# Eight key and value products of layer 1 moved into the end of layer 0's attention, and routing in one pass

## The chip, the cores and the metric

The kernel runs on one core of a Trainium2 chip. The metric is the time of one execution on the device in microseconds (us). TensorE is PE in the profile (PEld is its weight load), VectorE is DVE, ScalarE is ACT, GpSimd is POOL, and SyncE (SP) issues most DMAs.

## The reference

Two layers over 16 blocks (b = 0 to 15) of 128 tokens of width 512, all in float32. Each layer is a cross attention, added to the tokens, and then a mixture of eight experts of which each token takes two, added again.

```python
# layer 0
x = x + attention0(layernorm(x), ctx)      # fp8-rounded self attention and cross attention
t = layernorm(x)                           # written to x0_dram, what the experts read
probs = softmax(t @ Wg); gate, expert = top_k(probs, 2)
x = x + sum of gate * (relu(t[expert's tokens] @ w1) @ w2)      # at most 640 tokens an expert
# layer 1, per block b
h = layernorm(x[b])
k = concat(ctx[b] @ Wk, h @ Wk)            # 128 context rows, 128 own rows
v = concat(ctx[b] @ Wv, h @ Wv)
q = h @ Wq                                 # 16 heads of 128, four groups for k and v
k, q = rope(rms_norm(k)), rope(rms_norm(q))
x = x + softmax(q k^T / sqrt(128)) v @ Wo
x = x + two experts of eight on layernorm(x), weighted by softmax of the top two logits
```

`ctx` is an input: the products `ctx[b] @ Wk` and `ctx[b] @ Wv` of layer 1 depend on nothing that layer 0 makes.

## The kernel before

There are four stages, one after the other: layer 0's attention (0 to about 1368 us of the profiled execution), its experts (to 2408), layer 1's attention (to about 3474) and its experts (to 3819).

**Order.** Within a stage PE, DVE, ACT and POOL run in the order that the Python code is written in (`InOrder`, line 67, wraps every call; therefore nearly all instructions carry L67 in the profile). DMAs on SP are placed by the framework's scheduler. Tiles come from pools; a new tile waits until the memory that it gets is no longer used, also by tiles of a pool that was closed before.

**Layer 0's attention** (`Layer0`) goes over 64 token blocks n: four quarters (half of the heads of cross or self attention each) of 16 blocks. `ORDER` lists the steps of a period as (step, lag): step `name` of block n is issued in period n + lag, so that up to nine blocks are in flight. Steps are named by what they do: `Kp`, `Vp`, `Qp` project, `po0`, `po1` are the output projection into one PSUM bank, `xr` adds it to the tokens, `rn1` ... `rtb` are the routing steps. Weights are prepared in pieces into the pool tag `w`, 28 units of 4 KB per partition. After n = 63 the pipeline runs dry: in periods 64 to 71 fewer and fewer steps are left, at the end only routing.

**Routing** (`Routing`, lines 174 to 319) is the same in both layers. For each block of 128 tokens:
- `rl`, `rmx`, `rex`, `rch` (logits, top, exps, choice): logits on PE, then the two best experts and their weights on DVE, and a mask of 128 x 8.
- `rpl` (ranks): two small f32 matmuls, a triangle of ones (`before`) with the mask, and ones with `macc`, the masks of earlier blocks summed.
- `rsl` (slots): DVE makes each token's slot in its expert, and adds the mask to `macc`.
- `rlh` (onehots): `r_one` and `r_two` by six DVE operations of 128x128, for each of the two choices one for the slot's one half, and two for its other half, times the token's number and times its weight.
- `ren`, `rtb` (entry, entered): the matmul of `r_one` and `r_two`, 256 columns in f32 (token numbers and weights), added into `r_table` by DVE.

In layer 0 routing runs in quarter 3 alone; the last blocks are 60 to 63.

**Layer 0's experts** (`Experts0`) begin with `slot_rows` (line 924 on): DVE makes `e_ids`, `e_source` and `e_target` out of `r_table`. POOL then gathers the first expert's token blocks `g` by `e_source`, PE transposes them, and `h` (first matmul) and `o` (second) follow for eight experts. `rows_behind` sets `e_zero` and writes it to DRAM. Tiles for layer 1's weights (`c_wq`, `c_wk`, `c_wv`, `c_wo`) lie in a pool of their own; the list `ahead` loads them during the experts.

**Layer 1's attention** (`Layer1`) has its own list `ORDER1` with lags 0 to 8 over 16 blocks; a period takes about 64.2 us. `Kp0`/`Vp0` project the context's key and value (r = 0; `Kp1`/`Vp1` the tokens' own), each four f32 matmuls of 128x512; `Ksq0`, `Krs0`, `Kn0` normalise the key, `V0` copies the value from PSUM to SBUF. `AHEAD` issues these for b = 0 and 1 before period 0. In a period the order around the change is

```python
("QT0", 4), ("Qa1", 4), ("Vp0", 4), ("Qs1", 4), ("rn1", 6),
("sc10", 4), ("PT02", 5), ("pn3", 5), ("Kp0", 3), ("V0", 4), ("lnn", 3), ("sc00", 4),
("nm10", 4), ("rp1", 6), ("Ksq0", 3), ("trX", 3),
```

so Kp0 of block b runs in period b + 3, and Vp0 in period b + 4. `lnn` writes `xn` on DVE, and `trX` transposes it on PE.

Of the kernel before, what the change touches and what calls it, by code (L numbers as in the profile page):

```python
# [11 lines left out]
F32 = mybir.dt.float32  # L12
# [11 lines left out]
P = 128  # L24
# [32 lines left out]
class InOrder:  # L57


    def __init__(self, tc, engine):  # L60
        self.tc, self.engine = tc, engine
# [19 lines left out]
class Ops:  # L81


    def __init__(self, nc, tc, const):
        self.nc, self.tc, self.uid = nc, tc, 0
        self.ident = self.t(const, [P, P], F32, "ident")
        make_identity(nc, self.ident)
        self.ones = self.t(const, [P, P], F32, "ones")
        nc.gpsimd.memset(self.ones, 1.0)

        self.before = self.t(const, [P, P], F32, "before")
        nc.gpsimd.affine_select(
            out=self.before, in_=self.ones, pattern=[[1, P]], compare_op=ALU.is_gt,
            fill=0.0, base=0, channel_multiplier=-1,
        )
        self.iota = self.t(const, [P, P], F32, "iota")
        nc.gpsimd.iota(
            self.iota, pattern=[[1, P]], base=0, channel_multiplier=0,
            allow_small_or_imprecise_dtypes=True,
        )  # L100
        self.tok = self.t(const, [P, NB], F32, "tok")
        nc.gpsimd.iota(
            self.tok, pattern=[[P, NB]], base=0, channel_multiplier=1,
            allow_small_or_imprecise_dtypes=True,
        )
        self.tok1 = self.t(const, [P, NB], F32, "tok1")
        nc.gpsimd.iota(
            self.tok1, pattern=[[P, NB]], base=1, channel_multiplier=1,
            allow_small_or_imprecise_dtypes=True,
        )  # L110
        self.mhalf = self.t(const, [P, 16], F32, "mhalf")
        nc.gpsimd.memset(self.mhalf, -0.5)
# [33 lines left out]
class Router:  # L146
# [5 lines left out]

    def __init__(self, ops, pool, x_dram, w, probs, hi_first, rows, turned):
        nc = ops.nc
        self.ops, self.pool, self.x_dram = ops, pool, x_dram
        self.w, self.probs, self.hi_first = w, probs, hi_first

        self.rows, self.turned = rows, turned  # L160
        t = ops.t
        self.macc = t(pool, [P, E], F32, "r_macc")
        nc.gpsimd.memset(self.macc, 0.0)
        self.table = t(pool, [P, 2 * P], F32, "r_table")
        nc.gpsimd.memset(self.table, 0.0)
        self.weight = t(pool, [P, NB, 2], F32, "r_weight")
        self.expert = t(pool, [P, NB, 2], F32, "r_expert")
        self.pos = t(pool, [P, NB, 2], F32, "r_pos")
        self.onehot = t(pool, [P, NB, 2, E], F32, "r_onehot")
        self.base = t(pool, [P, E], F32, "r_base")  # L170
        nc.vector.tensor_scalar(self.base, ops.iota[:, :E], float(SPAN), None, ALU.mult)


class Routing:
# [61 lines left out]
    def choice(self):  # L236

        r, j, v, mx, s1 = self.r, self.j, self.v, self.mx, self.s1
        nc = r.ops.nc
        wt = r.weight[:, j, :]  # L240
        if r.probs:
            nc.vector.reciprocal(s1[:, 2:3], s1[:, 1:2])
            nc.vector.tensor_scalar(v, v, s1[:, 2:3], None, ALU.mult)
            nc.vector.max(mx, v)
            nc.vector.tensor_copy(wt, mx[:, 0:2])
        else:
            nc.vector.tensor_scalar(s1[:, 2:3], s1[:, 1:2], 1.0, None, ALU.add)
            nc.vector.reciprocal(wt[:, 0:1], s1[:, 2:3])
            nc.vector.tensor_tensor(wt[:, 1:2], s1[:, 1:2], wt[:, 0:1], ALU.mult)
        ix = self.tile([P, E], U32, "r_ix", 2)  # L250
        nc.vector.max_index(ix, mx, v)
        ex = r.expert[:, j, :]
        nc.vector.tensor_copy(ex, ix[:, 0:2])
        oh = r.onehot[:, j, :, :]
        for k in range(2):
            nc.vector.tensor_scalar(
                oh[:, k, :], r.ops.iota[:, :E], ex[:, k : k + 1], None, ALU.is_equal
            )
        self.mask = self.tile([P, E], F32, "r_mask", 2)
        nc.vector.tensor_tensor(self.mask, oh[:, 0, :], oh[:, 1, :], ALU.add)  # L260

    def ranks(self):
        ops = self.r.ops
        self.pp = ops.t(self.psum, [P, D], F32, "mm")
        ops.nc.tensor.matmul(self.pp[:, :E], ops.before, self.mask, start=True, stop=False)
        ops.nc.tensor.matmul(self.pp[:, :E], ops.ones, self.r.macc, start=False, stop=True)

    def slots(self):

# [22 lines left out]
    def onehots(self):  # L292
        r, j = self.r, self.j
        nc, iota = r.ops.nc, r.ops.iota
        first, second = (1, 0) if r.hi_first else (0, 1)
        self.one = self.tile([P, 2, P], F32, "r_one", 1)
        self.two = self.tile([P, 2, 2 * P], F32, "r_two", 1)
        for k in range(2):
            a, b = (self.lohi[:, i, k : k + 1] for i in (first, second))
            nc.vector.tensor_scalar(self.one[:, k, :], iota, a, None, ALU.is_equal)  # L300
            for i in range(2):
                by = r.weight[:, j, k : k + 1] if i else r.ops.tok1[:, j : j + 1]
                nc.vector.tensor_scalar(
                    self.two[:, k, i * P : (i + 1) * P], iota, b, by, ALU.is_equal, ALU.mult
                )

    def entry(self):
        r = self.r
        self.pt = r.ops.t(self.psum, [P, D], F32, "mm")
        for k in range(2):  # L310
            r.ops.nc.tensor.matmul(
                self.pt[:, : 2 * P], self.one[:, k, :], self.two[:, k, :],
                start=(k == 0), stop=(k == 1),
            )

    def entered(self):

        r = self.r
        r.ops.nc.vector.tensor_tensor(r.table, r.table, self.pt[:, : 2 * P], ALU.add)


def project(ops, psum, xT, w, cols):
# [14 lines left out]

WEIGHTS = ("k", "q0", "v", "q1", "p0", "p1")
BANKS0 = {"mm": 3, "tr": 2, "sc": 1, "pv": 1, "po": 1}

# [36 lines left out]
class Layer0:  # L377
# [9 lines left out]

    def __init__(self, ops, tc, args, x_dram, vec, router, small, wpool, work, dram, banks):  # L390
        self.plain, self.tc = ops.nc, tc
        ops.nc = Engines(tc, ops.nc)
        nc, t = ops.nc, ops.t
        self.ops, self.args, self.x_dram, self.vec, self.router = ops, args, x_dram, vec, router
        self.wpool, self.work, self.banks = wpool, work, banks

        self.kept = {
            kind: [t(dram, [P, D], F32, f"kept_{kind}{b}") for b in range(NB)]
# [249 lines left out]
    def load(self, n):  # L648
# [15 lines left out]
        if quarter in (1, 3):  # L664
            s["xq"] = t(work, [P, NC, P], F32R, "xq", 3)
            self.fetch("q" if quarter == 3 else "qx", b, s["xq"])

    def load_v(self, n):
        ops, t, s = self.ops, self.ops.t, self.at[n]
        quarter, b = divmod(n, NB)  # L670
# [205 lines left out]
    def run(self):  # L876
        lags = {name: lag for name, lag in ORDER}
        count = 0
        for period in range(4 * NB + max(lags.values())):
# [5 lines left out]
            for i, (name, lag) in enumerate(ORDER):  # L885
                if 0 <= period - lag < 4 * NB:
                    self.step(name, period - lag)
                count += 1
                if count % 3 == 0 and (period % NB < 7 or count % 2 == 0):
                    self.weight_step()  # L890
# [2 lines left out]
        self.ops.nc = self.plain  # L893


def layer0_attention(ops, tc, args, x_dram, vec, router):
    with ExitStack() as ctx:
        small = ctx.enter_context(tc.tile_pool(name="a_small", bufs=1))
        wpool = ctx.enter_context(tc.tile_pool(name="a_w", bufs=1))
# [5 lines left out]
            def tile(self, shape, dt, name, tag, bufs=None):  # L905
                return psum.tile(shape, dt, name=name, tag=tag, bufs=BANKS0[tag])

        Layer0(ops, tc, args, x_dram, vec, router, small, wpool, work, dram, Banks()).run()


def gather(ops, out, table, index):
# [289 lines left out]
class Layer1:  # L1201
# [8 lines left out]
    )  # L1210

    def __init__(self, ops, args, x_rows, w, rope_dram, router, out, first, work, banks):
        self.ops, self.args, self.x_rows, self.rope_dram = ops, args, x_rows, rope_dram
        self.first = first
        self.wq, self.wk, self.wv, self.wo = w
        self.router, self.out, self.work, self.banks = router, out, work, banks
        self.at = [{} for _ in range(NB)]
# [1 line left out]
    def load_first(self, b):  # L1219

        t, nc, s = self.ops.t, self.ops.nc, self.at[b]
        s["cT"] = t(self.first, [P, NC, P], F32, "cT", 2)
        nc.sync.dma_start(out=s["cT"], in_=self.args["ctxT"][b])
        s["rp"] = t(self.first, [P, 3, 2, P], F32, "rp", 3)
        nc.sync.dma_start(out=s["rp"].rearrange("p i s h -> p (i s h)"), in_=self.rope_dram[b])

# [82 lines left out]
    def key_step(self, name, r, b, s):  # L1309
        ops, nc, t = self.ops, self.ops.nc, self.ops.t  # L1310
        src = s["hT"] if r and name in ("Kp", "Vp") else s["cT"]
        if name == "Kp":
            s["ps", "k", r] = project(ops, self.banks, src, self.wk, slice(0, D))
        elif name == "Vp":
            s["vp", r] = project(ops, self.banks, src, self.wv, slice(0, D))
# [101 lines left out]
                self.at[period - last].clear()  # L1417


def layer1_attention(ops, tc, args, x_rows, w, rope_dram, router, out, first):  # L1420
    with ExitStack() as ctx:
        work = ctx.enter_context(tc.tile_pool(name="c_work", bufs=1))
        psum2 = ctx.enter_context(tc.tile_pool(name="c_ps", bufs=2, space=PSUM))
# [7 lines left out]
                return pool.tile(shape, dt, name=name, tag=tag)  # L1431

        scheduled, ops.nc = ops.nc, Engines(tc, ops.nc)
        Layer1(ops, args, x_rows, w, rope_dram, router, out, first, work, Banks()).run()
        ops.nc = scheduled


class Blocks1:
# [43 lines left out]
    def tables(self, small):  # L1482
# [4 lines left out]
        self.block0 = self.slots(small, ops.ident[:, 0:1], 1, "e0")  # L1487
        self.gather(0, self.at[0])
        pc = t(self.psum, [P, D], F32, "po")
        nc.tensor.matmul(pc[:, :E], ops.ones, router.macc, start=True, stop=True)  # L1490
        count = t(small, [P, E], F32, "count")

        nc.vector.tensor_scalar(count, pc[:, :E], 1.0, None, ALU.max)
# [149 lines left out]
def xattn_moe_two_layers(ctx: ExitStack, tc: tile.TileContext, args, out):  # L1643
# [21 lines left out]
    router0 = Router(ops, rpool0, x0_dram, wr[:, 0], True, False, ("xn", 2), ("lnT", 2))  # L1665
    router1 = Router(ops, rpool1, x1_dram, wr[:, 1], False, True, ("r_xn", 1), ("r_xT", 1))

    layer0_attention(ops, tc, args, x_rows, vec, router0)

    with tc.tile_pool(name="c_w", bufs=1) as wpool:  # L1670
        wq = t(wpool, [P, NC, NH * P], F32, "c_wq")
# [4 lines left out]
        def ahead(work):  # L1676
# [10 lines left out]

        layer0_experts(ops, tc, args, router0, x0_dram, x_dram, out, wpool, ahead)
        layer1_attention(
            ops, tc, args, x_rows, (wq, wk, wv, wo), rope_dram, router1, out, wpool  # L1690
        )
    layer1_experts(ops, tc, args, router1, x1_dram, out)

# [71 lines left out]
```

## Time and profile before

| | |
|---|---|
| median of three runs | 3816.66 us (3816.5 to 3819.55) |
| profiled execution | 3821.12 us, of which the span of the trace is 3819.4 |
| granted PE clock, mean | 0.971 |
| PE, DVE, ACT, POOL busy | 94%, 48%, 37%, 32% |
| layer 0's attention ends, e_ids starts | 1368.23 |
| first expert matmul h | 1388.42 |
| HBM traffic | 231.72 MB read, 78.92 MB written |

An f32 matmul is two instructions in the trace, an FP32R matmul one. A timeline line reads: start in us, duration in us, engine, line, operation, tile written <- tiles read, shape, count of like instructions in a row, and in brackets the engine's idle time before it with what ended it. The count of instructions and the busy time are given for each engine in the windows.

### The profile page before, as it was taken

What the parts mean: (1) busy time and instruction counts of PE and PEld (TensorE: products, weight loads), DVE (VectorE), ACT (ScalarE), POOL (GpSimd) and SP (SyncE); (2) the same over time, 40 slices, a digit from 0 to 9 for tenths busy, and PEclk for the clock granted to TensorE, in tenths of its full rate; (3) what the DMA queues carried; (4) which work ended last, traced back from release to release, by engine and by line L of the source; (5) the groups of instructions that cost most, each with busy time, mean ns of one, the idle gap of its engine ahead of it and who ended that gap; (6) DMA issues with size and microseconds to landing.
All of it is one profiled execution on the core that took longest, in us unless ns stands there. A gap on an engine that the chain in (4) does not pass through costs nothing. (4 is left out here: it accounts for less than half of the span.)

```text
span 3819.4 us, 42132 instructions
## 1 busy us (share of the span) xinstructions
PE 3597.5 (94%) x13349; PEld 2165.4 (57%) x13349; DVE 1838.0 (48%) x4269; ACT 1406.4 (37%) x5153; POOL 1214.3 (32%) x1487
## 2 busy tenths in 40 slices
PE   5999899889899869999999999899999999998998
PEld 3666566667688745444444444355555555554565
DVE  6888888778788923200000000255555555553111
ACT  5666555666676501101100000243434343441111
POOL 7546655654532202211001100332222222221332
PEclk8999899999899979999999999999999999998999
DMA  4333333333322163433233331200101010005333
GB/s 157 112 96 115 110 111 108 111 102 97 111 86 89 53 229 117 116 91 102 81 95 94 91 83 33 46 21 23 32 23 32 23 32 20 20 9 225 67 67 53
DMA packets 135412, 313.55 MB, mean 82 GB/s; under 512 B 15944, under 2 KB 16072, under 8 KB 133392
## 3 DMA queue, kind: packets, MB, share of 16 engines
q1 hardware_dynamic: 117488, 269.28, 21.9%
q0 software_dynamic: 17696, 41.43, 5.6%
q8 instruction: 119, 1.95, 0.2%
q14 instruction: 109, 0.89, 0.1%
HBM read 231.72 MB, written 78.92 MB: 81 GB/s over the span
## 5 line engine op out<-in xcount | busy, mean ns | idle before, releaser
L67 PE MATMUL h<-xT,w 128*128 128x512 f32 x1024 | 466.3, 595 | 5.1 <-PEq L1112 2.5
L67 PE MATMUL o<-w,hT 128*128 128x512 f32 x1024 | 460.8, 592 | 0.0
L67 ACT ACTIVATE hT<-h 128x512 f32<-128x512 f32 x128 | 76.3, 596 | 861.4 <-PE h L67 861.4
L67 DVE COPY xT<-tr 128x512 f32<-128x512 f32 x79 | 54.4, 688 | 593.9 <-PE tr L67 593.9
L67 PEld LDWEIGHTS o<-w,hT 128*128 128x128 f32 x1024 | 194.2, 190 | 243.7 <-issue 242.5
L67 PEld LDWEIGHTS h<-xT,w 128*128 128x128 f32 x1024 | 189.3, 190 | 233.3 <-issue 231.7
L67 PE MATMUL mm<-w,xq 128*128 128x512 f32 x1024 | 296.2, 434 | 24.5 <-DVE xq L67 7.0
L67 ACT ACTIVATE p<-sc,sm_nm 128x128 f32<-128x128 f32 (+1 forms) x768 | 300.9, 408 | 26.3 <-DVE sm_nm L67 15.7
L67 PE MATMUL sc<-kT,qT 128*128 128x128 f32 (+1 forms) x1536 | 267.6, 311 | 8.2 <-ACT p L67 5.5
L67 PE MATMUL pv<-pT,v 128*128 128x256 f32 (+1 forms) x768 | 258.5, 460 | 1.6 <-ACT pT L67 1.4
L67 PEld LDWEIGHTS sc<-kT,qT 128*128 128x128 f32 x1536 | 222.4, 191 | 66.3 <-issue 44.5
L67 ACT ACTIVATE hn_sq<-mm 128x128 f32<-128x128 f32 x768 | 213.2, 278 | 125.6 <-PE mm L67 104.9
L67 POOL DMA_INDIRECT x_dram<-y,e_target x40 | 62.9, 1574 | 574.7 <-ACT y L67 564.9
L67 PEld LDWEIGHTS mm<-w,xq 128*128 128x128 f32 x1024 | 199.0, 202 | 77.6 <-issue 10.0
L67 PE MATMUL mm<-c_wq,hT 128*128 128x512 f32 x512 | 231.2, 594 | 0.7 <-DVE qn L67 0.7
L67 PE MATMUL po<-c_wo,oT 128*128 128x512 f32 x512 | 231.4, 595 | 0.0
L67 DVE TENSOR_REDUCE sm_nm<-sc 128x4 f32<-128x512 f32 (+1 forms) x256 | 176.0, 687 | 114.0 <-PE sc L67 111.9
L67 POOL TENSOR_TENSOR hn_rs<-hn_rs,mhalf 128x4 f32<-128x4 f32 x192 | 202.8, 1056 | 16.0
L67 PE MATMUL h<-e_w,xT 128*128 (+1 forms) x624 | 201.8, 467 | 4.1 <-issue 3.3
L67 PE MATMUL po<-w,cq 128*128 128x512 f32 x512 | 184.2, 441 | 22.5 <-DVE cq L67 3.4
L67 POOL TENSOR_SCALAR hn_rs<-hn_ss,ws 128x4 f32<-128x4 f32 x160 | 70.1, 438 | 420.0 <-ACT hn_sq L67 419.7
L67 PE MATMUL tr<-ident,p 128*128 128x128 f32 x1024 | 157.1, 280 | 48.1 <-DVE p L67 40.8
(234 smaller groups left out, 6441.6 us busy)
## 6 DMA issues: line engine op xcount, KB each, us to landing
w<-in_f_w SPq DMA_DIRECT2D x128, 512.0 KB
x_dram<-xr SPq DMA_DIRECT2D x64, 256.0 KB
xr<-x_dram SPq DMA_DIRECT2D x64, 256.0 KB
e_w<-in_f_w SPq DMA_DIRECT2D x8, 1408.0 KB
xk<-in_ctxT SPq DMA_DIRECT2D x32, 256.0 KB
xv<-in_ctxT SPq DMA_DIRECT2D x32, 256.0 KB
raw<-in_wproj SPq DMA_DIRECT2D x32, 256.0 KB
lnT<-kept_lnT SPq DMA_DIRECT2D x32, 256.0 KB
```

Of the source, the lines that this page charges most:

```text
L67: return self.tc.keep_in_program_order(call(*args, **kwargs))
```

## The change

It has three parts.

1. **Early products.** When `Vp` of the last block of layer 0's attention has been issued, `load_early` loads Wk and Wv of layer 1 (four halves in `w` units) and the contexts of b = 2 to 5 (in the buffers `xk` and `xv`). `follow` then issues their eight products (K and V of four contexts) on PE behind steps of block 63: two after `po1`, one after `rl`, one after `rpl`, four after `ren`. Each is copied by ACT into a `v` tile and stored to `kv_dram` (256 KB) by SP.
2. **Layer 1** reads them back. For b = 2 to 5 Kp0 issues no matmul: the tile `cT` now holds the key product, loaded from DRAM, and Ksq0 and Kn0 read it from SBUF. Vp0 is a DMA straight into the tile `v`, and V0 does nothing.
3. **Routing in one pass**, in both layers. Mask, `macc`, `before` and ones of the ranks are bf16. `r_one` and `r_two` are FP32R. The weights are cut into two halves (two small DVE operations in `choice`), so `r_two` has 384 columns instead of 256. Its four weight one-hots are made on POOL; DVE keeps two for the token numbers and two for `r_one`. `entered` has a second DVE addition.

```diff
@@ Ops, Router
-        self.before = self.t(const, [P, P], F32, "before")
+        self.ones_b = self.t(const, [P, P], BF16, "ones_b")
+        nc.gpsimd.memset(self.ones_b, 1.0)
+        self.before_b = self.t(const, [P, P], BF16, "before_b")
...
-        self.macc = t(pool, [P, E], F32, "r_macc")
+        self.macc = t(pool, [P, E], BF16, "r_macc")
@@ Routing.choice
-        self.mask = self.tile([P, E], F32, "r_mask", 2)
+        self.mask = self.tile([P, E], BF16, "r_mask", 2)
...
+        half = self.halves = self.tile([P, 2, 2], F32, "r_halves", 2)
+        nc.vector.tensor_scalar(
+            half[:, 0, :].bitcast(U32), wt.bitcast(U32), 12, 12, ALU.logical_shift_right,
+            ALU.logical_shift_left,
+        )
+        nc.vector.tensor_tensor(half[:, 1, :], wt, half[:, 0, :], ALU.subtract)
@@ Routing.ranks
-        ops.nc.tensor.matmul(self.pp[:, :E], ops.before, self.mask, start=True, stop=False)
-        ops.nc.tensor.matmul(self.pp[:, :E], ops.ones, self.r.macc, start=False, stop=True)
+        ops.nc.tensor.matmul(self.pp[:, :E], ops.before_b, self.mask, start=True, stop=False)
+        ops.nc.tensor.matmul(self.pp[:, :E], ops.ones_b, self.r.macc, start=False, stop=True)
@@ Routing.onehots
-        self.one = self.tile([P, 2, P], F32, "r_one", 1)
-        self.two = self.tile([P, 2, 2 * P], F32, "r_two", 1)
+        self.one = self.tile([P, 2, P], F32R, "r_one", 1)
+        self.two = self.tile([P, 2, 3 * P], F32R, "r_two", 1)
...
+            nc.vector.tensor_scalar(
+                self.two[:, k, :P], iota, b, r.ops.tok1[:, j : j + 1], ALU.is_equal, ALU.mult
+            )
             for i in range(2):
-                by = r.weight[:, j, k : k + 1] if i else r.ops.tok1[:, j : j + 1]
-                nc.vector.tensor_scalar(
-                    self.two[:, k, i * P : (i + 1) * P], iota, b, by, ALU.is_equal, ALU.mult
+                nc.gpsimd.tensor_scalar(
+                    self.two[:, k, (i + 1) * P : (i + 2) * P], iota, b,
+                    self.halves[:, i, k : k + 1], ALU.is_equal, ALU.mult,
                 )
@@ Routing.entry, entered
-                self.pt[:, : 2 * P], self.one[:, k, :], self.two[:, k, :],
+                self.pt[:, : 3 * P], self.one[:, k, :], self.two[:, k, :],
...
+        weights = r.table[:, P:]
         r.ops.nc.vector.tensor_tensor(r.table, r.table, self.pt[:, : 2 * P], ALU.add)
+        r.ops.nc.vector.tensor_tensor(weights, weights, self.pt[:, 2 * P : 3 * P], ALU.add)
@@ Layer0
+EARLY = (2, 3, 4, 5)
+EARLY_AFTER = {"po1": 2, "rl": 1, "rpl": 1, "ren": 4}
...
+    def load_early(self):
+        nc, t = self.ops.nc, self.ops.t
+        assert not self.pieces and self.units >= 4
+        self.early_w, self.early = [], []
+        for w in (self.args["Wk"], self.args["Wv"]):
+            halves = [t(self.wpool, [P, 2, D], F32, "w", W_UNITS) for _ in range(2)]
+            for i, half in enumerate(halves):
+                nc.sync.dma_start(out=half, in_=w[:, 2 * i : 2 * i + 2, :])
+            self.early_w.append(halves)
+        for k, b in enumerate(EARLY):
+            cT = t(self.work, [P, NC, P], F32, "xv" if k % 2 else "xk", 2)
+            nc.sync.dma_start(out=cT, in_=self.args["ctxT"][b])
+            self.early += [(b, i, cT) for i in range(2)]
+
+    def early_product(self):
+        nc, t = self.ops.nc, self.ops.t
+        b, i, cT = self.early.pop(0)
+        ps = t(self.banks, [P, D], F32, "mm")
+        for c in range(NC):
+            nc.tensor.matmul(
+                ps, cT[:, c, :], self.early_w[i][c // 2][:, c % 2, :],
+                start=(c == 0), stop=(c == NC - 1),
+            )
+        out = t(self.work, [P, D], F32, "v", 3)
+        nc.scalar.copy(out, ps)
+        nc.sync.dma_start(out=self.kv_dram[b][i], in_=out)
+
+    def follow(self, name):
+        if name == "Vp":
+            self.load_early()
+        for _ in range(EARLY_AFTER.get(name, 0)):
+            self.early_product()
...
                     self.step(name, period - lag)
+                    if period - lag == 4 * NB - 1:
+                        self.follow(name)
@@ Layer1
+        early = self.kv_dram[b][0] if b in EARLY else None
+        if early is None:
+            nc.sync.dma_start(out=s["cT"], in_=self.args["ctxT"][b])
+        else:
+            nc.sync.dma_start(out=flat(s["cT"]), in_=early)
...
+        early = r == 0 and b in EARLY
+        if early and name == "Kp":
+            s["ps", "k", r] = flat(s["cT"])
+        elif early and name == "Vp":
+            if "v" not in s:
+                s["v"] = t(self.work, [P, 2, D], F32, "v", 3)
+            nc.sync.dma_start(out=s["v"][:, r, :], in_=self.kv_dram[b][1])
+        elif early and name == "V":
+            pass
+        elif name == "Kp":
             s["ps", "k", r] = project(ops, self.banks, src, self.wk, slice(0, D))
```

More of the change, by code (lines that the diff above doesn't have):

```diff
@@ L89, in __init__ @@
         nc.gpsimd.memset(self.ones, 1.0)
-        self.before = self.t(const, [P, P], F32, "before")
+        self.ones_b = self.t(const, [P, P], BF16, "ones_b")
+        nc.gpsimd.memset(self.ones_b, 1.0)
+        self.before_b = self.t(const, [P, P], BF16, "before_b")
         nc.gpsimd.affine_select(
-            out=self.before, in_=self.ones, pattern=[[1, P]], compare_op=ALU.is_gt,
+            out=self.before_b, in_=self.ones_b, pattern=[[1, P]], compare_op=ALU.is_gt,
             fill=0.0, base=0, channel_multiplier=-1,
@@ L377, with __init__ @@
 class Layer0:
-    def __init__(self, ops, tc, args, x_dram, vec, router, small, wpool, work, dram, banks):
+    def __init__(self, ops, tc, args, x_dram, vec, router, kv_dram, small, wpool, work, dram, banks):
         self.plain, self.tc = ops.nc, tc
@@ L394, in __init__ @@
         self.ops, self.args, self.x_dram, self.vec, self.router = ops, args, x_dram, vec, router
-        self.wpool, self.work, self.banks = wpool, work, banks
+        self.wpool, self.work, self.banks, self.kv_dram = wpool, work, banks, kv_dram
         self.kept = {
@@ L893, in run, with layer0_attention @@
         self.ops.nc = self.plain
-def layer0_attention(ops, tc, args, x_dram, vec, router):
+def layer0_attention(ops, tc, args, x_dram, vec, router, kv_dram):
     with ExitStack() as ctx:
@@ L906, in tile @@
                 return psum.tile(shape, dt, name=name, tag=tag, bufs=BANKS0[tag])
-        Layer0(ops, tc, args, x_dram, vec, router, small, wpool, work, dram, Banks()).run()
+        Layer0(
+            ops, tc, args, x_dram, vec, router, kv_dram, small, wpool, work, dram, Banks()
+        ).run()
 def gather(ops, out, table, index):
@@ L1210, with __init__ @@
     )
-    def __init__(self, ops, args, x_rows, w, rope_dram, router, out, first, work, banks):
+    def __init__(self, ops, args, x_rows, w, rope_dram, kv_dram, router, out, first, work, banks):
         self.ops, self.args, self.x_rows, self.rope_dram = ops, args, x_rows, rope_dram
-        self.first = first
+        self.first, self.kv_dram = first, kv_dram
         self.wq, self.wk, self.wv, self.wo = w
@@ L1222, in load_first @@
         s["cT"] = t(self.first, [P, NC, P], F32, "cT", 2)
-        nc.sync.dma_start(out=s["cT"], in_=self.args["ctxT"][b])
+        early = self.kv_dram[b][0] if b in EARLY else None
[3 more added lines that the diff above has]
+            nc.sync.dma_start(out=flat(s["cT"]), in_=early)
         s["rp"] = t(self.first, [P, 3, 2, P], F32, "rp", 3)
@@ L1311, in key_step @@
         src = s["hT"] if r and name in ("Kp", "Vp") else s["cT"]
-        if name == "Kp":
+        early = r == 0 and b in EARLY
[8 more added lines that the diff above has]
+        elif name == "Kp":
             s["ps", "k", r] = project(ops, self.banks, src, self.wk, slice(0, D))
@@ L1417, in run, with layer1_attention @@
                 self.at[period - last].clear()
-def layer1_attention(ops, tc, args, x_rows, w, rope_dram, router, out, first):
+def layer1_attention(ops, tc, args, x_rows, w, rope_dram, kv_dram, router, out, first):
     with ExitStack() as ctx:
@@ L1433, in layer1_attention @@
         scheduled, ops.nc = ops.nc, Engines(tc, ops.nc)
-        Layer1(ops, args, x_rows, w, rope_dram, router, out, first, work, Banks()).run()
+        Layer1(
+            ops, args, x_rows, w, rope_dram, kv_dram, router, out, first, work, Banks()
+        ).run()
         ops.nc = scheduled
@@ L1489, in tables @@
         pc = t(self.psum, [P, D], F32, "po")
-        nc.tensor.matmul(pc[:, :E], ops.ones, router.macc, start=True, stop=True)
+        nc.tensor.matmul(pc[:, :E], ops.ones_b, router.macc, start=True, stop=True)
         count = t(small, [P, E], F32, "count")
@@ L1666, in xattn_moe_two_layers @@
     router1 = Router(ops, rpool1, x1_dram, wr[:, 1], False, True, ("r_xn", 1), ("r_xT", 1))
-    layer0_attention(ops, tc, args, x_rows, vec, router0)
+    kv_dram = {b: [t(dram, [P, D], F32, f"early{b}{i}") for i in range(2)] for b in EARLY}
+    layer0_attention(ops, tc, args, x_rows, vec, router0, kv_dram)
     with tc.tile_pool(name="c_w", bufs=1) as wpool:
@@ L1689, in xattn_moe_two_layers @@
         layer1_attention(
-            ops, tc, args, x_rows, (wq, wk, wv, wo), rope_dram, router1, out, wpool
+            ops, tc, args, x_rows, (wq, wk, wv, wo), rope_dram, kv_dram, router1, out, wpool
         )
```

## The prediction

> **What bounds the kernel now.** I read the page first: busy totals, the chain, the 40 slices. Then the windows by stage, the timelines of PE and DVE around each place that the diff touches, and the idle time before PE's instructions.
>
> ```profile
> PE 3597.5 (94%) x13349; PEld 2165.4 (57%) x13349; DVE 1838.0 (48%) x4269; ACT 1406.4 (37%) x5153; POOL 1214.3 (32%) x1487
> PE   5999899889899869999999999899999999998998
> DVE  6888888778788923200000000255555555553111
> PE 34%; issue 1%; DVE 1%; DMA 0%; POOL 0%; ACT 0%; POOLq 0%; SPq 0%; ACTq 0%; DVEq 0%
> ```
>
> PE is the bound: 94% busy, and nearly all of the chain that is named. Two slices matter: late in layer 0's attention DVE stands at 9 while PE falls to 6. So the same microsecond of PE work has three prices, and the windows (span; sum; PE, PEld, DVE, ACT, POOL busy; clock; DMA share; GB/s) give them:
>
> ```profile
> 1140.00:1160.00 20.00, 19.70 (x113) 16.68 (x112) 18.17 (x61) 12.61 (x53) 5.34 (x8) 1.00 0.30 84
> 1340.00:1380.00 40.00, 16.55 (x60) 13.17 (x59) 19.16 (x91) 1.89 (x6) 5.00 (x6) 0.54 0.71 260
> 2500.00:3400.00 900.00, 899.33 (x3133) 501.32 (x3132) 475.95 (x1196) 365.99 (x1399) 250.30 (x368) 1.00 0.08 24
> ```
>
> Quarter 3 of layer 0: PE full, DVE at 91%. The tail: PE 41% busy at half clock (0.54). Layer 1: PE never waits.
>
> **1. Eight products put into the tail.** One product is four f32 128x512 matmuls, 3.44 us at full clock (c_wv,cT starts at 2946.55, the next instruction at 2949.99). 8 x 3.44 = 27.5 us of PE enter a stretch where PE idles some 23 of 40 us. What matters is whether they lie in that idle time. The tail now (start, duration):
>
> ```profile
> 1342.49 1.75 PE L67 MATMUL mm<-r_two,r_one 128*128 128x256 f32 x4
> 1352.15 1.08 PE L67 MATMUL tr<-ident,xn 128*128 128x128 f32 x4 [6.68 <-DVE xn L67]
> 1365.69 2.05 PE L67 MATMUL mm<-r_two,r_one 128*128 128x256 f32 x4 [2.43 <-DVE r_two L67]
> 1368.23 0.23 DVE L67 TENSOR_SCALAR e_ids<-r_table 128x128 f32<-128x128 f32 x1
> 1369.80 1.33 POOL L67 DMA_INDIRECT g<-x_dram,e_source  x1 [18.64 <-DMA inv<-in_inv_freq]
> 1377.92 1.09 PE L67 MATMUL tr<-ident,g 128*128 128x128 f32 x4 [10.18 <-DMA w<-in_f_w]
> 1388.42 1.91 PE L67 MATMUL h<-xT,w 128*128 128x512 f32 x2
> ```
>
> The gap of 10.18 looks made for the last four products. But in the changed kernel as built, e_ids waits for the last matmul of product 8, because its tile lies where the early Wv half lay. So do e_zero and the load of c_wk; the first gather waits for the last early store too. That gap is therefore behind the products and covers nothing. Step by step:
> - Products 1 and 2 stand between po1(63) and ren(60), from 1342.5; the clock is half there until about 1344, which adds 0.75: they end at 1350.1. DVE sits idle before rtb(60) (4.41 us, for PE), which waits for ren(60), and is in order: behind rtb(60) are queued rsl(61), xr(63), rmx(62) and all the rest. rtb(60) starts at 1350.7 instead of 1344.27; xr(63) at 1352.5 instead of 1345.94: +6.5, hidden by nothing.
> - trR(63) takes over that +6.5; ren(61) in one pass at half clock gives back some 1.4, so rl(63) ends at 1362.4 instead of 1357.3. Product 3 then runs beside rmx, rex, rch and the one-hots of block 62 (3.24 us of PE idle now), product 4 beside rsl(63) and its one-hots (2.43 idle now): all but about 1 us of the two is covered. ren(63) ends at about 1371.5 instead of 1367.7: +3.8.
> - Products 5 to 8: 4 x 3.44 = 13.8, nothing beside them: end X = 1385.3, e_ids +17.1.
> - The gather now starts 1.57 after e_ids. Behind product 8 come copy (0.59), the store and, ahead of it in SP's queue, c_wk of 1 MB (at 350 to 400 GB/s of this stretch, 2.6 to 3 us): 4 to 6 us, +2.5 to +4.4. Also behind them on SP: posi, inv, all of w1 and w2. The first expert weight is issued about X + 7, while the first h comes 20 us after e_ids: it lands in time. c_wv, c_wq, c_wo slide behind the weights into a stage with DMA share below 0.6: nothing.
> Sum: 17.1 + 3.5 = **+21 us** (15 if the store lands at once and P1, P2 find cover in DVE's queue; 27 if it lands as slowly as a gather, 7.8 us). ACT's 8 copies and the loads of Wk, Wv and ctxT (issued periods earlier, DMA share 0.1 to 0.3) cost nothing.
>
> **2. Eight products taken from layer 1.** Kp0 and Vp0 of b = 2 to 5 leave periods 5 to 9: at most 27.5. But trX needs xn, which DVE makes at an hour set by other PE work of the same period. The row that shows it: before steady state, period 4 has neither product, and PE waits
>
> ```profile
> 2461.93 1.99 PE L67 MATMUL sc<-kT,qT 128*128 128x256 f32 x8 [1.81 <-ACT qT L67]
> 2467.09 1.08 PE L67 MATMUL tr<-ident,xn 128*128 128x128 f32 x4 [3.17 <-DVE xn L67]
> ...
> 2630.92 0.54 DVE L67 TENSOR_SCALAR xn<-xn,ln_mv,ln_rs 128x512 f32<-128x512 f32 x1
> 2634.17 0.60 PE L67 MATMUL tr<-ident,xn 128*128 128x128 f32 x4
> ```
>
> 1.81 + 3.17 = 4.98 of the 6.88. The other way: period 7 has xn ready at 2631.60 (start + 0.68) and trX at 2634.17: a PE that is earlier by more than 2.57 waits, since xn's place on DVE follows from matmuls that stand before the removed ones. Read so, periods 5 to 9 give 1.18, 2.22, 2.57, 2.57, 2.49 = **-11** (bounds -9, period 4's 1.9 for each of five, and -27.5). The V0 copy that leaves ACT, and the four more 256 KB loads at DMA share 0.08, weigh nothing; K read from SBUF instead of PSUM is one DVE operation of equal shape, within 0.1.
>
> **3. Routing in one pass.** Entry: from four passes of 256 columns to two FP32R of 384. By-form row of the entry now, and its place:
>
> ```profile
> L67 PE MATMUL mm<-r_two,r_one 128*128 128x256 f32 x128 | 38.6, 430 | 8.0 <-DVE r_two L67 8.0
> 1296.25 1.03 PE L67 MATMUL mm<-r_two,r_one 128*128 128x256 f32 x4
> 1297.12 0.60 PE L67 MATMUL tr<-ident,p 128*128 128x128 f32 x4
> ```
>
> 0.87 us each. FP32R runs 512 columns in 0.244 (8 in 1.95 us at 1302.04), so 384 cost 0.18 to 0.27: 0.38 to 0.54. Ranks, 0.37 now, become about 0.17. Saved 0.5 to 0.72, I take 0.6.
> - Layer 1: 14 blocks in the PE-bound part x 0.6 = 8.4, and 0.5 in its tail: **-9** (-5 to -11; +0 of DVE's, it is at 53%).
> - Layer 0, quarter 3: ten periods of 18.44 (ren to ren) would fall to 17.84 on PE. DVE's busy time is 18.17/20 x 18.44 = 16.75; it gains the two halves (0.36) and the second add (0.26) and loses two one-hots (2 x 0.26): +0.10. To that comes contention with the four one-hots now on POOL. The nearest row:
>
> ```profile
> 1350.60 0.64 DVE L67 TENSOR_SCALAR r_one<-iota,r_lohi 128x128 f32<-128x128 f32 x1
> 1350.61 0.55 POOL L67 MEMSET e_zero<- 128x512 f32 x1
> ```
>
> The same r_one takes 0.28 at 1269.06; beside POOL 0.64, and it and the next one-hot move DVE on by 0.62 instead of 0.45. Four one-hots on POOL (some 0.35 each, between 0.23 for 128x4 and 0.70 for 128x512 bf16) at 0.17: 0.7; at the whole 0.36: 1.4; beside operations that feel nothing: 0. With 0.7, DVE's 17.55 and its waits of today (0.46 on sc, 0.59 on hn_rs) come up to PE's 17.84 or over it, so I take 0.45 of the 0.6: **-4.5** (-6 to +8, the latter rival C).
>
> The Trainium skill, page "SBUF — State Buffer", section "SBUF: two separate sides", says that DVE and GpSimd share a port pair as an exclusive lock: a DVE operation in a two-port mode, or with two SBUF inputs, and a GpSimd operation block each other for a whole instruction. The row shows a third of that (0.17 lost beside 0.55). The rule speaks against one-hots on POOL: by it each would hold up DVE for its whole length, 4 x 0.35 = 1.4 a period, and quarter 3 would go as in rival C.
>
> **Sum:** +21 - 11 - 9 - 4.5 = -3.5. The profiled execution took 3821.12 (span 3819.4), which is 4.5 above the median of the runs, 3816.66; the forecast is 3817.6 against the first and **3813** against the second. A measurement of this kernel tells about 0.2% (7.6 us) from no change, so this is no change.
>
> **Rivals.**
> - A, faster: no xn stall in layer 1, the full 27.5 is given back. For it: DVE is 53% busy there. Against: 3.17 in period 4. 3813 - 16.5 = 3797. Chance 0.15.
> - D, faster: the tail hides the products (D of +3). For it: 23 us of PE idle. Against: e_ids behind product 8. 3813 - 18 = 3795. Chance 0.09.
> - B, slower: PE stays at half clock through the products, as it does from 1350 to 1390 with PE half idle; then products 5 to 8 cost 27.5 instead of 13.8, 1 and 2 six more, 3 and 4 outgrow their cover by 3: +22, 3835. It makes the kernel slower from the second half-clock product on (3.44 each against 3.5), measurably from the fourth. Against: from 1388.42 steady work brings 1.00 within 4 us. Chance 0.14. The same holds if the stores and c_wk queue for over 20 us.
> - C, slower: DVE becomes the bound of quarter 3: 16.75 + 0.10 + 1.4 of contention + its waits of 1.05 = 19.3, 0.86 over today's 18.44, in ten periods +8 for -4.5, 3825. For it: 91% busy now. Against: the 0.17 of the row. Chance 0.14.
> - The forecast: 0.48; its own range is 3806 to 3821.
>
> Faster by over 0.2% (below 3809): A, D and 0.08 of the forecast, 0.32. Slower (above 3824.3): B, most of C and 0.04, 0.27. The rest 0.41. For 8 in 10, the range takes in half of A, and C, up to 3831; below 3796 and above it lie some 0.05 and 0.13.
>
> **What would show it.** In the profile after: e_ids near 1381 (its 1368.23 plus 17, less 4.5), first h 21 after its old time less 4.5 (1405); PE idle before trX, named DVE xn, of about 4 in periods 6 to 8 of layer 1; ren to ren 18.0 in quarter 3, with DVE above 95% busy there; one-hots on POOL of 0.35 to 0.7. I am wrong on item 1 if e_ids stands within 8 us of its old place, on item 2 if PE is over 99% busy in periods 5 to 9, on item 3 if the period is above 18.44.

## The result, and the profile after

The changed kernel takes 3833.34 us (median of five, 3832.0 to 3836.24) against 3816.66: 1.0037 of the time before, 95% interval 1.0025 to 1.0049. It is slower by 16.7 us; 3813 was forecast, with a range up to 3831. The profiled execution took 3832.0 (span 3830.3), the fastest of the five, and that of before, 3821.12, lies near the top of its kernel's runs (3816.5 to 3821.43); so the two traces differ by 10.9 us only. What follows compares these two traces, and uses medians for verdicts.

The busy totals, and the windows of the tail and of layer 1 that answer to those of before:

```profile
PE 3576.7 (93%) x13220; PEld 2141.8 (56%) x13220; DVE 1838.4 (48%) x4301; ACT 1406.4 (37%) x5157; POOL 1313.4 (34%) x1616
```

```profile
1340.00:1380.00 40.00, 29.61 (x77) 15.18 (x76) 15.08 (x78) 4.62 (x11) 10.11 (x13) 0.74 0.12 47
2500.00:3400.00 900.00, 884.93 (x3072) 492.16 (x3071) 482.46 (x1227) 371.40 (x1434) 298.19 (x429) 0.99 0.08 25
```

PE has 21 us less to do, and yet the kernel is longer. The tail is fuller (PE 74% busy instead of 41%), but its DMA share fell from 0.71 to 0.12: the loads that used to run beside the routing are gone from there. Layer 1, where PE never waited, now has 15 us of idle time and a clock of 0.99.

The timeline of PE from po1(63) to the first expert matmul, and the starts of e_ids (DVE) and of the first gather (POOL):

```profile
1337.61 7.03 PE L67 MATMUL mm<-w,xk 128*128 128x512 f32 x16
...
1356.42 6.13 PE L67 MATMUL mm<-w,xv 128*128 128x512 f32 x8
1366.12 1.11 PE L67 MATMUL mm<-r_two,r_one 128*128 128x384 f32 x2 [3.57 <-DVE r_two L67]
...
1373.23 7.03 PE L67 MATMUL mm<-w,xk 128*128 128x512 f32 x16
1380.09 7.03 PE L67 MATMUL mm<-w,xv 128*128 128x512 f32 x16
...
1412.77 1.09 PE L67 MATMUL tr<-ident,g 128*128 128x128 f32 x4 [3.65 <-DMA g<-x_dram,e_source]
...
1415.55 1.92 PE L67 MATMUL h<-xT,w 128*128 128x512 f32 x2
```

```profile
1387.16 0.23 DVE L67 TENSOR_SCALAR e_ids<-r_table 128x128 f32<-128x128 f32 x1 [12.99 <-PE mm L67]
```

```profile
1395.85 1.26 POOL L67 DMA_INDIRECT g<-x_dram,e_source  x1 [8.00 <-DMA x_dram<-e_zero]
```

The first 7.03 are products 1 and 2; the 6.13 is product 3 alone, at half clock; the two of 7.03 are products 5 to 8, and no gap is left between the last entry and them. e_ids waited 12.99 us for PE (13.8 was forecast for the four products); the gather then waited 8 us more.

The time at which the tail begins varies by up to 3.4 us from execution to execution (trR of block 62 stands at 1335.93 and 1339.34 in two kernels that are the same up to there, e1 and e9 below). So the tail is best timed from that step as a mark (1339.41 before, 1335.68 after). In us from that mark:

| step | before | after | later by | forecast |
|---|---|---|---|---|
| trR(63) | 12.7 | 17.2 | 4.5 | 6.5 |
| ren(62) | 21.1 | 30.4 | 9.3 | about 5 |
| ren(63) | 26.3 | 36.8 | 10.5 | 3.8 (its end) |
| e_ids | 28.8 | 51.5 | 22.7 | 17.1 |
| first gather | 30.4 | 60.2 | 29.8 | 20.6 |
| first h | 49.0 | 79.9 | 30.9 | 21 |

From the first h to layer 1's first trX nothing changed (1047.98 and 1048.24). From that trX to the sixteenth, layer 1 took 903.9 before and 889.3 after.

### The profile page after: what moved, and what is told of

It is laid out like the page before. It is cut to its first block, busy times and chain, and to the rows that moved or that the text cites. A ratio compares the mean times of both kernels' runs of the same rounds, so it can differ in the third digit from the quotient of the medians.

```text
span 3830.3 us, 42092 instructions
## 1 busy us (share of the span) xinstructions
PE 3576.7 (93%) x13220; PEld 2141.8 (56%) x13220; DVE 1838.4 (48%) x4301; ACT 1406.4 (37%) x5157; POOL 1313.4 (34%) x1616
## 5 line engine op out<-in xcount | busy, mean ns | idle before, releaser
L67 PE MATMUL mm<-w,xk 128*128 128x512 f32 x544 | 204.0, 519 | 2.3 <-DVE low_any L67 2.3
L67 PE MATMUL po<-w,cq 128*128 128x512 f32 x512 | 183.3, 439 | 22.7 <-DVE cq L67 3.4
```

The costliest lines, as they stand in the source:

```text
L67: return self.tc.keep_in_program_order(call(*args, **kwargs))
```

## The experiments

The theory after the two traces: the transition costs 31 us, because product 3 stops the routing through ACT, because products 5 to 8 are on the way to e_ids, and because the last store, c_wk and e_zero's stores fall between e_ids and the gather; layer 1 gives little back, because of the stall before trX and of the half clock that follows it. The rival: the places of the products don't matter, and the price lies in the longer use of layer 0's weight memory, or in the routing.

All runs, with the three parts of the transition (from trR of block 62) and layer 1 from the first to the sixteenth trX; "before" was run again with each group, at 3817.4, 3818.7 and 3818.1:

| kernel | median | to e_ids | e_ids to gather | gather to h | layer 1 |
|---|---|---|---|---|---|
| before | 3816.7 | 28.8 | 1.6 | 18.6 | 903.9 |
| after | 3833.3 | 51.5 | 8.7 | 19.7 | 889.3 |
| e1_routing_only | 3802.7 | 25.8 | 1.5 | 17.8 | 894.7 |
| e2_early_only | 3845.3 | 55.1 | 8.4 | 19.0 | 897.7 |
| e3_copy_late | 3823.2 | 47.1 | 8.2 | 19.0 | 887.6 |
| e4_no_last_four | 3816.8 | 38.4 | 7.6 | 18.9 | 888.5 |
| e5_xn_early | 3813.2 | 51.7 | 8.3 | 19.0 | 871.4 |
| e6_gaps4 | 3798.5 | 29.1 | 1.5 | 17.1 | 888.4 |
| e7_gaps4_xn | 3791.4 | 29.1 | 1.5 | 16.6 | 882.3 |
| e8_gaps6_xn | 3793.8 | 28.7 | 6.4 | 18.2 | 876.7 |
| e9_routing_xn | 3804.3 | 25.8 | 1.5 | 17.8 | 893.8 |
| e10_onehots_dve | 3807.4 | 27.6 | 1.6 | 18.3 | 894.7 |
| e11_gaps6_held | 3789.1 | 28.7 | 1.6 | 18.9 | 877.0 |
| e12_gaps4_tail | 3795.2 | 28.0 | 1.6 | 19.2 | 882.4 |

**The two halves.** The routing alone is the change without its hunks on EARLY and kv_dram; the early products alone are those hunks without the rest.

> Only the routing part of the change; no early products, layer 1 projects all its keys and values itself. Theory from the trace after: layer 0 gains 0.19 us in each of ten periods and some 2 us before them, layer 1 gains 0.83 us a block: 3816.7 - 4 - 13 = 3800, first h at about 1385. By the figures of the prediction (4.5 and 9): 3803. Rival: the 2 us that layer 0 gained ahead of its routing come from the early part; then 3802.

> Only the early products and layer 1's reading of them, with the routing of before. Theory from the trace after: the transition costs 31 us, or a few more since the old entries run at half clock there; layer 1 gives back 5: 3843 to 3847. By the prediction (21 and 11): 3827.

3802.7, ratio 0.9958 (0.9944 to 0.9972), and 3845.3, ratio 1.0075 (1.0061 to 1.0089). The change is a gain of 15 and a loss of 28. The first is where the prediction's figures put it (3803), but by luck: 12.2 and 2 instead of 9 and 4.5, as shown below; the second is within its theory. Against the routing alone, the products make the transition 34.9 us longer (79.9 against 45.0) and layer 1 5.4 shorter.

**Product 3 and ACT.** The copy is issued later in ACT's order:

```diff
-            self.early_product()
+            self.keep = self.early_product()   # returns copy and store, to be called
+            if name != "rl":
+                self.keep()
...
+        if name == "rex":
+            self.keep()
```

> The changed kernel, but ACT's copy of product 3 is issued behind the exps of block 63 instead of ahead of them. Theory: exps waited on ACT behind that copy for the whole of product 3 (6.13 us); now the entry of block 62 waits for product 3 on PE alone: e_ids 3.5 us earlier (1383.7), 3830. Rival: it is the half clock of product 3 alone that cost; then e_ids within 1 us of 1387.2.

ACT and DVE in the changed kernel, then ACT in this one:

```profile
1362.59 0.59 ACT L67 COPY v<-mm 128x512 f32<-128x512 f32 x1 [7.95 <-PE mm L67]
1363.07 0.27 ACT L67 ACTIVATE r_v<-mm,r_s 128x8 f32<-128x8 f32 x1
```

```profile
1363.47 0.16 DVE L67 RECIPROCAL r_s<-r_s 128x1 f32<-128x1 f32 x1 [6.70 <-ACT r_v L67]
```

```profile
1357.87 0.27 ACT L67 ACTIVATE r_v<-mm,r_s 128x8 f32<-128x8 f32 x1 [2.23 <-DVE r_s L67]
...
1363.68 0.58 ACT L67 COPY v<-mm 128x512 f32<-128x512 f32 x1 [5.45 <-PE mm L67]
```

The exps of block 63 (r_v) needed only its logits, but stood behind a copy that waited for product 3; DVE stood still for 6.70 us. With the copy behind them they ran at once, and e_ids came at 1383.76, 4.4 us earlier from the mark. ren(62) came no earlier (31.3 from the mark against 30.4): it now stands right behind product 3, which took 5.7 us here. The transition as a whole is 5.6 shorter, and layer 1 1.6, for a reason given below. The median fell by 10.1, the trace by 8.9; the eleven runs of this kernel spread from 3821.3 to 3833.5, so the difference of the medians is rough.

**Products 5 to 8.**

```diff
-EARLY = (2, 3, 4, 5)
-EARLY_AFTER = {"po1": 2, "rl": 1, "rpl": 1, "ren": 4}
+EARLY = (2, 3)
+EARLY_AFTER = {"po1": 2, "rl": 1, "rpl": 1}
```

> The changed kernel with two contexts (b = 2, 3) early instead of four: the four products behind the entry of block 63 are gone, layer 1 projects b = 4, 5 itself. Theory: these four cost their 13.8 us and the late start of gather and weights behind them, 8 us: first h at 1394, layer 1 gives back 2 us less: 3814. By the prediction: 13.8 + 3.5 less in the transition, 5 less given back: 3821.

From the mark to the first h 64.8, 15.0 less: the four products' 13.1 to e_ids, and 1.9 behind it. That the late start behind e_ids would go too was wrong: 7.6 us are left, though the last product now stands ahead of the last entry. And layer 1 took 888.5, not longer but 0.8 shorter than with four contexts: contexts 4 and 5 gave nothing back at all.

Of the 34.9 us by which the transition is longer than with routing alone, 13.1 are then products 5 to 8 (e4), 4.4 the order on ACT (e3), 7.2 the later gather and 1.9 what follows it. The 8.3 that are left are products 1 to 4 in PE's own order, if e3 and e4 may be added; no run takes these apart.

**The stall before trX.** One step of ORDER1 moves:

```diff
-("V0", 4), ("lnn", 3), ("sc00", 4)
+("V0", 4), ("sc00", 4)
...
-("Qn1", 4), ("ex03", 5)
+("Qn1", 4), ("lnn", 3), ("ex03", 5)
```

> The changed kernel with one step of layer 1 moved in its written order: lnn, which makes xn on DVE, stands behind Qn1 instead of behind V0, some 4.5 us earlier in the period. Theory: the stalls of 3.2 us before trX in periods 5 to 8, and the half clock that follows each, are what ate the relief; without them layer 1 gives 27 instead of 5 for the eight products: 3833 - 20 = 3813 (bounds 3811 and 3820), no wait for xn from period 5 on. Rival: the next wait takes its place (the scores wait for ACT's qT, 1.8 us in period 4); then 3823 or more.

> Routing alone, with lnn moved; no early products. It says how much of the gain of lnn's move is there without the products. Theory: only period 4, which has no context products in any kernel, loses its stall of 3.2 us: 3802.7 - 3 = 3800. Rival: the move is worth much by itself; then 3795 or less.

3813.2: 20 us faster than the changed kernel, by an order alone. Without the products the same move gave nothing (3804.3 against 3802.7; layer 1 893.8 against 894.7), so the theory of that run, 3800, missed: of the 3.3 us saved up to the second trX, 2.4 were lost again up to the third. So with xn early the eight products give 893.8 - 871.4 = 22.4 us back of their 27.5; without it 5.4. PE in a period of the changed kernel, and in the same period with lnn moved:

```profile
2589.55 1.99 PE L67 MATMUL sc<-kT,qT 128*128 128x256 f32 x8 [0.68 <-ACT qT L67]
2594.72 1.09 PE L67 MATMUL tr<-ident,xn 128*128 128x128 f32 x4 [3.18 <-DVE xn L67]
...
2596.45 5.57 PE L67 MATMUL mm<-c_wq,hT 128*128 128x512 f32 x8
```

```profile
2587.85 0.60 PE L67 MATMUL tr<-ident,xn 128*128 128x128 f32 x4
...
2588.72 3.60 PE L67 MATMUL mm<-c_wq,hT 128*128 128x512 f32 x8
```

The stall is 3.18, and behind it the transposes take 1.09 instead of 0.60 and a projection 5.57 instead of 3.60. The windows give the granted clock (the third column from the end): first a stretch of the changed kernel behind the stall and the whole period, then the same period in the kernel with the late copy, whose layer 1 is the same program:

```profile
2596.00:2600.00 4.00, 4.00 (x9) 1.93 (x8) 1.42 (x3) 3.22 (x11) 1.41 (x2) 0.50 0.74 240
...
2594.72:2657.99 63.27, 59.41 (x202) 33.23 (x203) 33.33 (x87) 25.42 (x98) 21.09 (x31) 0.96 0.10 32
```

```profile
2589.00:2650.00 61.00, 57.02 (x204) 32.13 (x205) 33.84 (x88) 25.42 (x98) 21.63 (x31) 0.99 0.10 33
```

The same stall of 3.17 to 3.19 us sometimes halves the clock for three to six us and sometimes hardly does. Here that is 63.3 against 60.5 us for a period. With lnn moved, the clock of these periods is 1.00.

**The places of the products.** EARLY_AFTER gives way to steps of chosen blocks; copies and stores are collected and issued behind `rch` (or `rpl`):

```diff
+EARLY = (2, 3)
+EARLY_AT = {("rl", 60): 1, ("rl", 61): 1, ("rl", 62): 2}
...
+        for _ in range(EARLY_AT.get((name, n), 0)):
+            self.early_product()           # appends copy and store to self.late
+        if n >= 4 * NB - 4 and name in ("rch", "rpl"):
+            while self.late:
+                self.late.pop(0)()
```

> Two contexts early (b = 2, 3), as in the run without the last four, but the four products stand where PE waits for DVE: one behind the logits of block 60, one behind those of 61, two behind those of 62 (the gap of 6 to 7 us before trR of block 63); ACT's copies are issued behind rch. Theory: the place is what costs. From trR of block 62 to the first h 46 us (45.0 with routing alone, 64.8 with the same four products in their old place); 3798. Rival: the price lies in the weights' pool, held longer whatever the place, so that c_wk and e_zero load later; then 5 to 8 us more, 3804.

3798.5. The same four products that cost 19.9 us in their old places (64.8 against 45.0 with routing alone) cost 2.7 here (47.7). Their copies on ACT moved with them. Two of the four stand ahead of the mark, where they cost nothing either: from trR of block 60 (1305.53 in both traces) to the mark it is 30.4 us with routing alone and 29.9 here. The rival falls: with the last of them done by 1350 the weights' pool is free in time, c_wk is loaded from 1350.13, and the gather starts 1.5 us after e_ids.

> The kernel before this one in this list (four products in the gaps) with lnn moved as well. Theory: all of the four products' 13.8 us are given back in layer 1 instead of 6: 3798 - 7.5 = 3790. Rival (another wait takes over): 3796 or more.

3791.4, ratio 0.9933 (0.9919 to 0.9946): 893.8 - 882.3 = 11.5 of the four products' 13.8 come back.

**The late pool.** Three contexts, with `("rl", 63): 1` and `("rpl", 63): 1` added to EARLY_AT:

> As the kernel before this one in this list, with three contexts: two more products, one behind the logits of block 63 (copied behind rch), one behind the ranks of block 63. Theory: layer 1 gives 20.6 us; the two later products are hidden by waits of 3.7 and 4.8 us, but the weights' pool is free some 15 us later and c_wk, e_zero load beside the gather, 5 us: 3788. Rival: the late pool costs 8 or more, as with the four old places: 3793.

The two more products are hidden (28.7 us to e_ids, as with four), and layer 1 gains 5.6; but the gather waits 6.4 us after e_ids instead of 1.5. The median, 3793.8, is at the rival's figure, but not clearly different from that of four products (ratios 0.9932 and 0.9933 to before). Then the same with the loads of layer 1's weights held back:

```diff
+            def load(out, in_):
+                ops.nc.vector.tensor_copy(out[:, 0, 0:1], nw[:, 0:1])
+                nc.sync.dma_start(out=out, in_=in_)
...
-            return calls + [lambda a=a: nc.sync.dma_start(out=a[0], in_=a[1]) for a in loads]
+            return calls + [lambda a=a: load(*a) for a in loads]
```

> Six products in the gaps and lnn moved, as before, and the loads of layer 1's weights (c_wk and the others) are held back by a DVE write into their tiles until the first expert runs, so that no 1 MB load stands ahead of the last early store and of e_zero's. Theory: the gather waits for the landing of that store behind c_wk: it starts 3 instead of 6.35 us after e_ids, 3794 - 4 = 3790. Rival: the store lands no sooner, because e_zero's five stores share the engines with it: gather within 1 us of 6.35 after e_ids, 3793.

SP's DMAs around the last early store, in the changed kernel; then the same with POOL's first gather, with six products and with the loads held:

```profile
1387.20 0.33 SPq L1762 DMA_DIRECT2D c_wk<-in_Wk  x1
1387.81 0.32 SPq L715 DMA_DIRECT2D early<-v  x1
```

```profile
1362.52 0.33 SPq L1768 DMA_DIRECT2D c_wk<-in_Wk  x1
1363.13 0.32 SPq L717 DMA_DIRECT2D early<-v  x1
```

```profile
1371.89 1.26 POOL L67 DMA_INDIRECT g<-x_dram,e_source  x1 [7.08 <-DMA x_dram<-e_zero]
```

```profile
1361.72 0.33 SPq L1291 DMA_DIRECT2D cT<-in_ctxT  x1
1362.33 0.32 SPq L717 DMA_DIRECT2D early<-v  x1
```

```profile
1366.39 1.27 POOL L67 DMA_INDIRECT g<-x_dram,e_source  x1 [2.37 <-DVE e_part L67]
```

The profile names e_zero's stores as what the gather waited for; in the built program it waits for the early stores, and not for e_zero's. With the 1 MB of c_wk (and then e_zero's stores) around the last early store, the gather starts 8.8 us after that store's issue (8.0 in the changed kernel); without c_wk 4.1, and then the store is no longer what it waits for. 3789.1, ratio 0.992 (0.9906 to 0.9933), is the lowest median of the study, 29 us below the runs of before in its group and 44 below the change; it is not clearly apart from that of four products with lnn moved (0.9919 to 0.9946).

**The one-hots.** All of them on DVE, with routing alone (`nc.gpsimd.tensor_scalar` in `onehots` becomes `nc.vector.tensor_scalar`):

> Routing alone, but the four weight one-hots of a block stand on DVE instead of POOL. Theory: DVE bounds quarter 3 since the change (period 18.24, DVE waits 0.54 of it); 4 x 0.26 = 1.04 more on DVE make the period 19.2 to 19.3, 10 us in ten periods, while the last blocks gain 2 to 4 us since they no longer wait for POOL's 0.8 us one-hots; layer 1 stays at 63.37 a block: 3809. Rival (what POOL and DVE take from each other is as large as what moves): the period stays within 0.3 of 18.24, 3800.

This theory fell, although the median, 3807.4, came near its 3809. Quarter 3's period is 18.29 us against 18.24, and layer 1 is the same to 0.1; the last blocks, which should have gained 2 to 4, lost 1.8 up to e_ids. DVE's busy time rose by only 0.6 us a period (122.47 of 128.02 us in seven periods against 118.41 of 127.67). By form, POOL's one-hots in the whole of the changed kernel, then one of DVE's two kinds in these seven periods, with routing alone and with all on DVE:

```profile
L67 POOL TENSOR_SCALAR r_two<-iota,r_lohi,r_halves 128x128 fp32r<-128x128 f32 x128 | 106.3, 841 | 126.6 <-DVE r_lohi L67 121.8 <-DVE r_s L67 4.8
```

```profile
L67 DVE TENSOR_SCALAR r_two<-iota,r_lohi,tok 128x128 fp32r<-128x128 f32 x14 | 6.3, 449 | 0.0
```

```profile
L67 DVE TENSOR_SCALAR r_two<-iota,r_lohi,tok 128x128 fp32r<-128x128 f32 x14 | 4.8, 342 | 0.0
```

Beside POOL's, DVE's one-hots took 0.449 (r_two) and 0.364 (r_one) in quarter 3, with all on DVE 0.342 and 0.280: 2 x 0.107 + 2 x 0.084 = 0.38 a block is what sharing cost. In layer 1 DVE's one-hots come after POOL's and lose nothing (0.340 and 0.279). What sets 18.24, with DVE at 93% and PE waiting 0.47 a period for qn from DVE, stays open.

**POOL in the last blocks.** In e1 the last entry waits for POOL:

```profile
1358.76 0.69 PE L67 MATMUL mm<-r_two,r_one 128*128 128x384 f32 x1 [3.94 <-POOL r_two L67]
```

So the weight one-hots of layer 0's last four blocks went to DVE, in the kernel of e7 (`late = not r.hi_first and j >= NB - 4`, and then `nc.vector`):

> Four products in the gaps and lnn moved, as before; the weight one-hots of layer 0's last four blocks are on DVE. Theory: the entries of blocks 62 and 63 wait for POOL's one-hots (3.94 + 0.86 us before the last): 2 to 4 us off the way to e_ids, 3791.4 - 3 = 3788. Rival: DVE has them no sooner; 3791.

Inconclusive: e_ids came 1.2 earlier, but the first h 1.5 later (48.7 against 47.2 from the mark), and 3795.2 (0.9924 to 0.9951) is not clearly different from e7.

## Why the prediction was wrong, point by point

| term | forecast | measured |
|---|---|---|
| transition | +21 | +30.9 |
| products taken from layer 1 | -11 | -5.4 |
| routing in layer 1 | -9 | -12.2 (9.2 to the sixteenth trX, 3 behind it, both from e1) |
| routing in quarter 3 | -4.5 | -2 (18.44 to 18.24 in ten periods) |
| sum | -3.5 | +11.3; the traces differ by 10.9, the medians by 16.7 |

- **Step "product 3 runs beside rmx, rex, rch"** failed. It counted PE and DVE, and left out that the product's own copy is queued on ACT ahead of `rex`. The change's ACT copies were costed at nothing; this one held the chain for 6.7 us, and moving it was worth 4.4 (e3). Nor was the product itself covered: with its copy moved, ren(62) still came right behind it.
- **The clock**, which was only a rival (B), was half true: products 3 and 4 took 6.1 and 5.3 us instead of 3.44 (the granted clock was 0.50 from 1350 to 1356.4, where PE was 55% busy, and 0.59 and 0.57 over these two), products 1, 2 and 5 to 8 ran at full clock. B's price of 22 was too high, its mechanism was there.
- **Products 5 to 8 lie on the way to e_ids**: right. 12.99 us of DVE's wait, 13.1 gone when they go (e4). The reason given was wrong: by the addresses of the built program, which no trace shows, e_ids does not lie where an early weight lay (e_zero does, over a half of the early Wk). Its pool takes the place of layer 0's weight pool, and each such wait in the built program (e_ids, e_zero, c_wk) covers the last use of the whole old pool. So c_wk, issued at 1347.21 before, moved behind the last product wherever that stood (1387.20 after, 1362.52 in e8).
- **The gather**: +2.5 to +4.4 was forecast, 7.1 measured. The copy, the store and c_wk were counted, c_wk at 2.6 to 3 us; e_zero's five stores were not. e11 shows c_wk's part: 4.7 us. Whether e_zero's stores have a part is not shown. The weights w came late too, but the gather bound the first h, as forecast (the last transpose before it waited 3.65 for g).
- **The relief of layer 1**: the stall on xn was right, and its size nearly (about 4 was forecast for periods 6 to 8; 2.14, 3.18, 3.19, 3.19 before trX in periods 5 to 8). What failed is the step "Read so, periods 5 to 9 give 1.18, 2.22, 2.57, 2.57, 2.49": it took PE's work behind the stall at full clock. The clock of periods 5 to 8 was 0.99, 0.96, 0.97 and 0.98 of 59.0, 63.3, 62.5 and 62.3 us, a loss of 6.2 us, where e1 and e5 have 1.00; 11.0 - 6.2 = 4.8, against the 5.4 measured. The rows that the prediction quoted for period 4 showed it: a trX of 1.08 behind a stall of 3.17, and 0.60 in the others. Rival A (no stall) was wrong as a forecast, and nearly right as soon as lnn moved (e5: 22.4 of 27.5).
- **Routing**: in layer 1 entries added 0.35 to PE's time (from the start of the projection ahead of them to the start of the scores behind them 3.79, less the projection's 3.44) and ranks 0.06, so a block saved 0.83 there instead of 0.6. In quarter 3 the step "I take 0.45 of the 0.6" failed: PE's busy time fell by 0.66 a period, but its waits rose from 0.30 to 0.77, so the period fell by 0.2. DVE's busy time is 16.90 a period, not 17.55, and 93%, not above 95%.
- **POOL's one-hots** take 0.84 us, not 0.35; that was an estimate between rows of other operations. Contention with DVE was put at 0.7 a period and is 0.38. The rule of the Trainium skill that the prediction weighed (page "SBUF — State Buffer", section "SBUF: two separate sides": a DVE operation in a two-port mode or with two SBUF inputs and a GpSimd operation block each other for a whole instruction) would give, as an estimate with the measured length, up to 4 x 0.84 = 3.4 a period; quarter 3 shows 0.38. Whether DVE's one-hots are operations of that kind, no run here shows. Rival C fell with it.
- **The 40 slices** were misread: DVE's 9 and PE's 6 stand in neighbouring slices, not in one (where PE is at 6, DVE is at 2). Nothing in the sum rests on it.
- **Rival B as the slower side** had 0.14, and the range ended at 3831, 2.3 below the result: the clock (rival B) and a late store (27 for the transition) were each thought of alone, ACT's order not at all, and none of the sum's bounds held two of them at once.

## What to carry to other kernels

Work that fills an engine's idle time has to be followed through all engines: its copy, its store and the pool that it keeps alive each stand in somebody's queue, and here one copy in ACT's queue cost 4.4 us and the late gather 7.2, beside the 13.1 of the four products that lay on the critical chain themselves. The place is worth more than the work: the same four products cost 19.9 us behind steps of the critical chain, and 2.7 where PE waited for another engine anyway, their copies moved along. Before work is taken off a full engine, find what it will wait for next and move that first: one line in DVE's order turned 5.4 us of relief into 22.4.

## What was not expected of the hardware

A stall of PE of 3.17 to 3.19 us was enough to halve its clock, sometimes, and with up to 6 us at half clock behind it (0.50 from 2596 to 2600) it cost up to nearly twice its own length: the same program took 63.3 and 60.5 us for the same period. The Trainium skill, page "TensorE: Matmul & The Clock Gate", section "HAM oscillation — how this bites in real kernels", asks for no gaps over some 3.4 us. The section "What's actually happening" of the same page says that the window runs freely, which agrees with the scatter; the runs here show that a gap a little below the rule's figure can be too long. A short wait of 0.68 us stands 2 us ahead of it; whether it has a part in this is not shown.
